# Local transformer: score masks written by ScalarE, and value windows read from a transposed copy of the state in DRAM

## The chip, the cores and the metric

The kernel runs on one core of one Trainium2 chip. The metric is the device time of one execution in microseconds (us), given as the median of three runs. Engines are named as in the profile: PE (TensorE, with its weight loader PEld), DVE (VectorE), ACT (ScalarE), POOL (GpSimd) and SP (SyncE, which only issues DMAs here).

## The reference

A model of two blocks over 16 sequences of 256 tokens with 128 channels, in f32. Block 0 has a linear attention and then, as its "ffn", a local transformer of six layers; block 1 has an attention with a position bias and a gelu MLP. The change lies in the local transformer:

```python
for i in range(6):                       # DEPTH
    x = attn_layer(shift_tokens(x), Wqkv[i], q_scale[i], k_scale[i], Wo[i]) + x
    x = ffn_layer(shift_tokens(x), ln_g[i], ln_b[i], W1[i], b1[i], W2[i], b2[i]) + x

def local_attention(q, k, v):            # 16 heads of 64, windows of 32 tokens
    bq, bk, bv = (t.reshape(b, h, n // 32, 32, 64) for t in (q, k, v))
    bk2, bv2 = look(bk), look(bv)        # own window and the one before: 64 keys
    mask = (it < jb) | (it > jb + w) | (jb == -1)
    sim = jnp.einsum('bhwie,bhwje->bhwij', bq, bk2) * 8.0
    sim = jnp.where(mask, -jnp.finfo(sim.dtype).max, sim)
    return jnp.einsum('bhwij,bhwje->bhwie', jax.nn.softmax(sim, -1), bv2)
```

Ahead of it q and k are divided by their norms, scaled and rotated; behind it the heads are multiplied by Wo and added to x.

## The kernel before, in words

There are three stages: the linear attention (0 to about 263 us), the local transformer (about 265 to 3640 us), and block 1 (from 3641 us). In the second stage the state lies transposed in SBUF: channels on the partitions, tokens along the row. A *unit* is two sequences; there are 8 units (`NU`), 6 layers (`DEPTH`), and each unit and layer is done in 4 iterations (`QS`), of four heads each: 192 iterations (`N`) of one loop (L1050 to L1129). It is a software pipeline: iteration n works on several lags at once.

For PE, ACT, DVE and POOL the order is the order of the code (`manual_schedule`); SP's DMAs, all in one queue, are ordered by the scheduler. In an iteration PE does, in order:

- `merging` (L927): output of iteration n-9 times the product of Wv and Wo (`vos`), 32 matmuls into the bank `y`; after the fourth of a unit the result is added to the state;
- `norms_rows` (L774, odd n): one transpose that turns the inverse norms of k into rows; ACT copies them out (`rkT`, L776), and a DMA brings them to DRAM (`rkh`);
- the steps of the feed-forward of an earlier unit (`ffn`, from L953 on, called through `behind`); its three gelus (L991) run on ACT at n%4 = 2, with a table load ahead of them and another ahead of the next exponentials;
- `flipped(p, 0)` (L888): four transposes of probabilities of iteration n-5; ACT copies them out (`prT`, L896);
- `windows` (L805), when n%4 = 3 for sequence s = 0 and when n%4 = 1 for s = 1: eight transposes of 64 tokens each, in steps of 32, so that the overlapping key blocks of 64 lie on partitions 0 to 63; ACT (L812) and DVE (L810) copy four each, and a DMA of 256 KB (L813) doubles them onto partitions 64 to 127;
- `masked` (L821): two matmuls of an identity with the bf16 mask, which open the two PSUM banks (`sim`) that the scores of iteration n-4 are added to;
- `flipped(p, 1)` (L888; DVE copies, L894);
- `norms_sum` (L722, even n): sums of squares of q and k; ACT copies them out (`n2`, L731);
- `weighted` (L906): 16 matmuls of windows and probabilities of iteration n-8; ACT and DVE copy out (`zx`, L921, L919);
- `scores` (L843): 128 small matmuls of iteration n-4 into the two `sim` banks; DVE takes the maxima (L855, L857);
- `norms_inverse` (L740, even n; the inverse square root runs on POOL, L758 to L766);
- `project` (L698): four matmuls for q and k of iteration n, each followed by a square on ACT (L701) and two DVE operations (L703, L706).

ACT interleaves with these the 16 exponentials of iteration n-4 (L865, with bias -max and an accumulated sum): eight for x = 0 between the squares, eight for x = 1 behind them. POOL divides by the sums (`divided`, L880, for x = 0 and x = 1), scales k by its inverse norms (`scaled`, L795) and adds the rotated halves (`rotate`, L714), which SP's eight `got` DMAs per iteration (L708, L709) bring. `widened` loads the inverse norms, spread over 64 partitions, as `kn` (four DMAs per iteration). PSUM has four banks for general use (`bank()`, named `mm`), three for `sim`, one for `y`. In the last iterations of a layer the next layer's Wq and Wk are loaded (`wqk`) and Wv and Wo multiplied (`merged`, L669 on).

Of the kernel before, what the change touches and what calls it, by code (L numbers as in the profile page):

```python
# [10 lines left out]
F32 = mybir.dt.float32  # L11
# [7 lines left out]
B, L, D = 16, 256, 128  # L19
NU = B // 2  # L20
# [4 lines left out]
WIN = 32  # L25
PAD = WIN
# [18 lines left out]
def adaln_kernel(  # L45
# [5 lines left out]
    nc = tc.nc  # L51
# [6 lines left out]
    def bank():  # L58
        return stage["ps"].tile([128, 512], F32, tag="mm", name="mm")
# [48 lines left out]
    zs = []  # L108
# [129 lines left out]
    with block:  # L238
# [98 lines left out]
        def upright(rows):  # L337

            pt = bank()
            for t in range(4):  # L340
                nc.tensor.transpose(pt[:, t * 128 : (t + 1) * 128], rows[:, t, :], ident)
            return pt
# [257 lines left out]
    with ExitStack() as es:  # L600
# [12 lines left out]
        def persistent(tag, shape, dtype=F32):  # L613
            t = lc.tile(list(shape), dtype, tag=tag, name=tag)
            nc.gpsimd.memset(t, 0.0)
            return t
# [7 lines left out]
        nc.sync.dma_start(sel, io["c_sel"])  # L624

        ks = [persistent(f"k{j}", (128, 2, PAD + L)) for j in range(8)]
        rope = lc.tile([128, 2, 2, L], F32, tag="rope", name="rope")
        nc.sync.dma_start(rope, io["c_rope"].rearrange("p (j a) t -> p j a t", j=2))

# [164 lines left out]
            k = ks[m % 8][:, :, PAD:]  # L794
            nc.gpsimd.tensor_tensor(k, k, two(kn), ALU.mult)  # L795

        def windows(u, s):


            xw = atile("xw", (128, 8, 128))  # L800
            for g in range(2):
                pt = bank()
                for j in range(4):
                    w0 = 32 * (4 * g + j)
                    nc.tensor.transpose(  # L805
                        pt[0:64, j * 128 : (j + 1) * 128], zs[u][:, s, w0 : w0 + 64], ident
                    )
                dst = xw[0:64, 4 * g : 4 * g + 4, :].rearrange("p w d -> p (w d)")
                if g:
                    nc.vector.tensor_copy(dst, pt[0:64, :])  # L810
                else:
                    nc.scalar.copy(dst, pt[0:64, :])  # L812
            nc.sync.dma_start(xw[64:128], xw[0:64])  # L813
            return xw

        def masked():

            sims = []
            for par in range(2):
                sim = pss.tile([128, 512], F32, tag="sim", name="sim")  # L820
                nc.tensor.matmul(  # L821
                    sim,
                    ident16,
                    maskb.unsqueeze(1).to_broadcast([128, 2, 256]),
                    start=True,
                    stop=False,
                    skip_group_check=True,
                )
                sims.append(sim)
            return sims  # L830

        def scores(sims, m, qs):

# [216 lines left out]
        while n < N + 9 or behind:  # L1050
            layer, at_ = divmod(n, per)
            if at_ == 13 and 0 < layer < DEPTH:
                wffs[layer] = load_ffn(layer)
            if 0 <= n - 4 < N:
                for m in (2 * (n - 4), 2 * (n - 4) + 1):
                    scaled(m, kns.pop(m))

            w, j = divmod(n - 9, QS)
            if 0 <= w < DEPTH * NU:
                if j == 0:  # L1060
                    pys[w] = psy.tile([128, 512], F32, tag="y", name="y")
                merging(j, zxs.pop((w, j)), vos[w // NU], pys[w])
                if j == QS - 1:
                    add_to_state(w % NU, pys.pop(w))
            if n % 2 and 3 <= n <= N + 1:
                home = norms_rows(rk)
            go_on(behind)
            go_on(merges)
            if 0 <= n - 1 < N:
                for m in (2 * (n - 1), 2 * (n - 1) + 1):  # L1070
                    rotate(m, qs[m], got.pop(m))
            if 0 <= n - 5 < N:
                i, u, p = place(n - 5)
                if p == 0:
                    prTs[i, u] = atile("prT", (128, NP, 512))
                flipped(p, 0, prs[n - 5], prTs[i, u])
            for s, lag in ((0, 7), (1, 9)):
                v, r = divmod(n - lag, QS)
                if r == 0 and 0 <= v < DEPTH * NU:
                    xws[v, s] = windows(v % NU, s)  # L1080
            sims = masked() if 0 <= n - 4 < N else None
            if 0 <= n - 5 < N:
                flipped(p, 1, prs.pop(n - 5), prTs[i, u])

            if n % 2 == 0 and 2 <= n <= N:
                n2 = norms_sum([squares.pop(m) for m in range(2 * n - 4, 2 * n)])
            v, r = divmod(n - 8, QS)
            if 0 <= v < DEPTH * NU:
                zxs[v, r] = weighted(r, xws[v, r // 2], prTs[v // NU, v % NU])
            go_on(behind)  # L1090
            if sims:
                m = 2 * (n - 4)
                rn = inverses[m // 4][:, m % 4 // 2]
                scores(sims, m, [qs.pop(m), qs.pop(m + 1)])
                pr = atile("pr", (128, 2, 4, 2, 64), 1)
                nbs = [maxima(sims[par], rn[:, par]) for par in range(2)]
                ssum = small("ssum", (128, 2, 4, 2))

            if n % 2 == 0 and 2 <= n <= N:
                rk, inverses[n // 2 - 1] = norms_inverse(n2)  # L1100
            if 0 <= w < DEPTH * NU and j == QS - 1:
                behind.append(ffn(w % NU, w // NU))
            go_on(behind)
            between = exponentials(0, sims, nbs, rn, pr, ssum) if sims else iter(())
            for m in (2 * n, 2 * n + 1):
                if n < N:
                    i, u, p = place(n)
                    qs[m], squares[m], got[m] = project(i, u, m, wqk[p + m % 2], between)
                if m % 2 == 0:
                    go_on(behind)  # L1110
            if sims:
                for x in range(2):
                    for _ in between:
                        pass
                    divided(pr[:, x], ssum[:, x])
                    between = exponentials(1, sims, nbs, rn, pr, ssum) if x == 0 else iter(())
                prs[n - 4] = pr
            if 0 <= n - 3 < N:
                for m in (2 * (n - 3), 2 * (n - 3) + 1):
                    kns[m] = widened(m, home)  # L1120
            if layer + 1 < DEPTH:
                if at_ == 18:
                    merges.append(merged(layer + 1))
                if at_ > per - QS:
                    p = 2 * (at_ - (per - QS) - 1)
                    wqk[p : p + 2] = [load_qk(layer + 1, p), load_qk(layer + 1, p + 1)]
            if at_ == 0 and 0 < layer < DEPTH:
                wqk[NP - 2 :] = [load_qk(layer, NP - 2), load_qk(layer, NP - 1)]
            n += 1  # L1129
# [468 lines left out]
```

## Time and profile before

| what | value |
| --- | --- |
| median of 3 runs (lowest to highest) | 4208.09 us (4206.36 to 4209.53) |
| the profiled execution: its time, its span | 4207.77 us, 4206.0 us |
| mean granted TensorE clock | 0.981 |
| second stage, 265 to 3640 us: busy PE, DVE, ACT, POOL | 3205.6, 2326.9, 2266.9, 2262.6 us of 3375 |
| PE on the windows' transposes (L805), one of 64 x 128 | 768, of about 0.11 us each when they follow each other |
| PE on the masks (L821) | 384, of 0.215 us each when they follow each other |
| DMA `xw<-xw` | 96 of 256 KB |

A line of the timeline gives start, duration, engine, line, operation, output <- inputs, partitions x elements, count, and in brackets how long the engine had been idle and what released it. In a line of groups the numbers after the bar are busy time and mean duration in ns of one, and after the next bar the idle time just before these instructions with its releaser. The granted clock is that of PE, 1.00 at full speed.

### The profile page before, as it was taken

How to read it: one execution, taken by the hardware profiler on the slowest of the kernel's cores; microseconds unless marked ns; L12 is line 12 of the kernel's file. 1: busy time of each engine (PE TensorE's matmuls, PEld its weight loads, DVE VectorE, ACT ScalarE, POOL GpSimd, SP SyncE). 2: the span in 40 equal slices, each digit the busy share in tenths (PEclk: the TensorE clock that was granted, in tenths of full speed). 3: DMA queues.
4: the chain of work that ended last, by engine and by line, in shares of the span. 5: the costliest groups of instructions: out<-in, count | busy, mean ns of one | idle time of the engine just before them, and what ended most of it. 6: DMA issues, size and time to landing. Idle time of an engine off the chain costs nothing.

```text
span 4206.0 us, 118202 instructions
## 1 busy us (share of the span) xinstructions
PE 3938.9 (94%) x45491; PEld 2580.1 (61%) x45491; DVE 2856.0 (68%) x6005; ACT 2753.1 (65%) x9640; POOL 2655.1 (63%) x3374
## 2 busy tenths in 40 slices
PE   7877999999999999999999999999999999799998
PEld 4534666666666666666666666666666666455554
DVE  6746767677767767676777777776767675476664
ACT  4535666667666666667666667666666766276665
POOL 5446666776666676666676766767666665155453
PEclk9878999999999999999999999999999999899999
DMA  1333444444444444444444444444434442200000
GB/s 41 41 90 97 106 109 105 109 107 105 106 105 114 104 110 105 105 110 102 111 109 105 112 103 106 108 110 105 110 100 105 104 105 72 64 1 6 9 3 11
DMA packets 193547, 371.06 MB, mean 88 GB/s; under 512 B 42537, under 2 KB 83416, under 8 KB 192984
## 3 DMA queue, kind: packets, MB, share of 16 engines
q1 hardware_dynamic: 192984, 363.50, 34.3%
q8 instruction: 360, 5.90, 0.6%
q14 instruction: 203, 1.66, 0.1%
HBM read 127.92 MB, written 8.91 MB: 33 GB/s over the span
## 4 chain that ended last, share of the span: by engine, by line
PE 46%; DVE 22%; ACT 19%; issue 7%; POOL 5%; DMA 1%; SPq 0%; POOLq 0%; DVEq 0%; ACTq 0%
ACT pr L865 11%; PE mm L906 9%; PE sim L843 7%; DVE sent L703 6%; ACT sq L701 4%; PE mm L722 4%; PE mm L888 4%; POOL pr L880 4%; DVE k L706 3%; DVE q L706 3%; PE mm L698 3%; DVE mx L855 3%; PE mm L805 2%; PE mm L1376 2%; PE sim L1303 2%
## 5 line engine op out<-in xcount | busy, mean ns | idle before, releaser
L865 ACT ACTIVATE pr<-sim,nb,rq 128x64 f32<-128x64 f32 x3072 | 1229.5, 454 | 336.8 <-DVE nb L857 318.3
L880 POOL TENSOR_TENSOR pr<-pr,rsum 128x512 f32<-128x512 f32 x384 | 398.3, 1042 | 807.3 <-DVE rsum L878 761.8
L865 ACT ACTIVATION_READ_ACCUMULATOR pr<-sim,nb,rq 128x1 f32 x3072 | 784.5, 255 | 0.0
L927 PEld LDWEIGHTS y<-zx,wvo 128*128 128x128 f32 x6144 | 716.1, 192 | 92.1 <-issue 89.0
L927 PE MATMUL y<-zx,wvo 128*128 128x128 f32 x6144 | 717.7, 275 | 1.3 <-ACT zx L921 1.2
L698 PE MATMUL mm<-z,wqk 128*128 128x512 f32 x1536 | 706.9, 602 | 8.6 <-DMA wqk<-in_L_ffn_Wqkv_dram 6.7
L703 DVE SCALAR_TENSOR_TENSOR sent<-mm,vec,rope 128x512 f32<-128x512 f32 x768 | 570.4, 743 | 118.2 <-ACT sq L701 110.2
L714 POOL TENSOR_TENSOR q<-q,got 128x512 f32<-128x512 f32 x384 | 488.3, 1272 | 12.7 <-DMA got<-sent 10.2
L714 POOL TENSOR_TENSOR k<-k,got 128x512 f32<-128x512 f32 x384 | 496.2, 1292 | 0.0
L795 POOL TENSOR_TENSOR k<-k,kn 128x512 f32<-128x512 f32 x384 | 481.9, 1274 | 17.9 <-DMA kn<-rkh 17.9
L701 ACT ACTIVATE sq<-mm 128x512 f32<-128x512 f32 x768 | 475.7, 619 | 23.3 <-PE mm L698 23.3
L698 PEld LDWEIGHTS mm<-z,wqk 128*128 128x128 f32 x1536 | 278.7, 192 | 322.9 <-issue 234.7
L919 DVE COPY zx<-mm 128x512 f32<-128x512 f32 x384 | 265.6, 692 | 262.0 <-PE mm L906 262.0
L921 ACT COPY zx<-mm 128x512 f32<-128x512 f32 x384 | 224.9, 586 | 287.0 <-PE mm L906 287.0
L906 PE MATMUL mm<-prT,xw 64*128 64x256 f32 x3072 | 389.7, 391 | 3.8 <-DVE zx L919 2.0
L855 DVE TENSOR_REDUCE mx<-sim 128x8 f32<-128x512 f32 x384 | 263.1, 685 | 171.9 <-PE sim L843 171.9
L906 PEld LDWEIGHTS mm<-prT,xw 64*128 64x128 f32 x3072 | 293.5, 187 | 121.7 <-issue 92.2
L1346 POOL TENSOR_TENSOR pr<-pr,rsum 128x256 f32<-128x256 f32 (+1 forms) x256 | 205.1, 832 | 241.7 <-DVE rsum L1344 218.3
L888 PE MATMUL mm<-ident,pr 128*128 128x128 f32 x1536 | 244.6, 282 | 105.1 <-POOL pr L880 75.9
L888 PEld LDWEIGHTS mm<-ident,pr 128*128 128x128 f32 x1536 | 174.9, 142 | 270.0 <-POOL pr L880 240.6
L843 PEld LDWEIGHTS sim<-k,q 64*32 64x32 f32 x24576 | 265.8, 105 | 83.3 <-issue 55.2
L843 PE MATMUL sim<-k,q 64*32 64x64 f32 x24576 | 299.7, 226 | 15.9 <-POOL k L795 8.1
(253 smaller groups left out, 6461.5 us busy)
## 6 DMA issues: line engine op xcount, KB each, us to landing
got<-sent SPq DMA_DIRECT2D x1536, 128.0 KB
kn<-rkh SPq DMA_DIRECT2D x768, 128.0 KB
xw<-xw SPq DMA_DIRECT2D x96, 256.0 KB
wqk<-in_L_ffn_Wqkv_dram SPq DMA_DIRECT2D x48, 128.0 KB
bhome<-brow SPq DMA_DIRECT2D x1, 3072.0 KB
wv<-in_L_ffn_Wqkv_dram SPq DMA_DIRECT2D x12, 256.0 KB
wo<-in_L_ffn_Wo_dram SPq DMA_DIRECT2D x12, 256.0 KB
xt<-in_x_dram SPq DMA_DIRECT2D x8, 256.0 KB
```

Source lines behind the costliest of these rows:

```text
L698: nc.tensor.matmul(pp, wqk[:, j, :], xs, start=True, stop=True)
L701: nc.scalar.activation(sq, pp, AF.Square)
L703: nc.vector.scalar_tensor_tensor(two(sent[:, j, :]), two(pp), scale, tab[1], ALU.mult, ALU.mult)
L714: nc.gpsimd.tensor_tensor(r, r, two(got[:, j, :]), ALU.add)
L795: nc.gpsimd.tensor_tensor(k, k, two(kn), ALU.mult)
L843: nc.tensor.matmul(sims[par][32 * c : 32 * c + 32, c0 : c0 + 64], q[r, s, t0 : t0 + 32], k[r, s, t0 : t0 + 64], start=False, stop=True, sk ...
L855: nc.vector.tensor_reduce(mx, sim.rearrange("p (b k) -> p b k", b=8), AX.X, ALU.max)
L865: nc.scalar.activation(pr[:, x, st, par, :], sims[par][:, b * 64 : (b + 1) * 64], AF.Exp, bias=nbs[par][:, b : b + 1], scale=rn[:, par, b ...
L880: nc.gpsimd.tensor_tensor(prf, prf, rsum.unsqueeze(2).to_broadcast([128, 8, 64]), ALU.mult)
L888: nc.tensor.transpose(pt[:, st * 128 : (st + 1) * 128], pr[:, x, st].rearrange("p h k -> p (h k)"), ident,)
L906: nc.tensor.matmul(pz[par][:, w * 256 : (w + 1) * 256], xw[r, (2 * k + w) % 8, :], prT[r, :, 64 * k + 32 * w : 64 * k + 32 * w + 32], star ...
L927: nc.tensor.matmul(py[:, j * 128 : (j + 1) * 128], vo[:, h, :], zx[:, h % 2, h // 2, :], start=(h == 0), stop=(h == 2 * NP - 1), skip_grou ...
```

## The change

Two things change in the second stage.

*Masks.* `masked` now handles one `sim` bank per call, and only the first three calls of all (the ring's three banks) use the matmul; the other 381 are an ACT copy of the bf16 mask into the bank, and the scores are added to what lies there. It is called one iteration ahead of the scores: the first bank behind `flipped(p, 1)` (on ACT: behind the prT copy and ahead of n2 and zx), the second at the end of the iteration (on ACT: behind all exponentials, ahead of the next iteration's rkT, gelu and prT work).

*Windows.* Once per unit and layer (n%4 = 3) `upright` transposes the state of both sequences by four 128x128 transposes into one bank, ACT copies it out, and two DMAs of 128 KB write it as rows into a DRAM buffer (one of two, by unit), behind 32 rows of zeros. `windows` then makes no transposes: four DMAs of 128 KB per sequence read the overlapping blocks of 64 rows straight onto both halves of the partitions. In `before` a unit has sixteen transposes, two ACT and two DVE copies and two DMAs for it. A memset and four small DMAs at the stage's start write the zeros.

In the built order of SP, the loads of `kn` in the iteration n%4 = 3 change place too: three of the four now come behind the eight `got` DMAs, where before they alternated.

```diff
--- before.py
+++ after.py
@@ -624,6 +624,13 @@
         nc.sync.dma_start(sel, io["c_sel"])
 
         ks = [persistent(f"k{j}", (128, 2, PAD + L)) for j in range(8)]
+
+        rows = [dr.tile([2, PAD + L, D], F32, tag=f"rows{j}", name=f"rows{j}") for j in range(2)]
+        zero = work("zero")[0:PAD, 0:D]
+        nc.vector.memset(zero, 0.0)
+        for home in rows:
+            for s in range(2):
+                nc.sync.dma_start(home[s, 0:PAD, :], zero)
         rope = lc.tile([128, 2, 2, L], F32, tag="rope", name="rope")
         nc.sync.dma_start(rope, io["c_rope"].rearrange("p (j a) t -> p j a t", j=2))
 
@@ -794,40 +801,48 @@
             k = ks[m % 8][:, :, PAD:]
             nc.gpsimd.tensor_tensor(k, k, two(kn), ALU.mult)
 
-        def windows(u, s):
+        def upright(u, home):
+
+            pt = bank()
+            for t in range(4):
+                s, c = t // 2, PAD + 128 * (t % 2)
+                nc.tensor.transpose(
+                    pt[:, t * 128 : (t + 1) * 128], zs[u][:, s, c : c + 128], ident
+                )
+            xt = work("xt").rearrange("p (s h d) -> p s h d", s=2, h=2)
+            nc.scalar.copy(xt.rearrange("p s h d -> p (s h d)"), pt)
+            for s in range(2):
+                nc.sync.dma_start(
+                    home[s, PAD : PAD + L, :].rearrange("(h p) d -> p h d", p=128), xt[:, s]
+                )
+
+        def windows(s, home):
 
 
             xw = atile("xw", (128, 8, 128))
-            for g in range(2):
-                pt = bank()
-                for j in range(4):
-                    w0 = 32 * (4 * g + j)
-                    nc.tensor.transpose(
-                        pt[0:64, j * 128 : (j + 1) * 128], zs[u][:, s, w0 : w0 + 64], ident
-                    )
-                dst = xw[0:64, 4 * g : 4 * g + 4, :].rearrange("p w d -> p (w d)")
-                if g:
-                    nc.vector.tensor_copy(dst, pt[0:64, :])
-                else:
-                    nc.scalar.copy(dst, pt[0:64, :])
-            nc.sync.dma_start(xw[64:128], xw[0:64])
+            for r in range(0, 128, WIN):
+                t0 = r % (2 * WIN)
+                nc.sync.dma_start(
+                    xw[r : r + WIN],
+                    home[s, t0 : t0 + L, :].rearrange("(w p) d -> p w d", p=WIN),
+                )
             return xw
 
+
+
+        banks = []
+
         def masked():
 
-            sims = []
-            for par in range(2):
-                sim = pss.tile([128, 512], F32, tag="sim", name="sim")
+            sim = pss.tile([128, 512], F32, tag="sim", name="sim")
+            src = maskb.unsqueeze(1).to_broadcast([128, 2, 256])
+            if len(banks) < 3:
                 nc.tensor.matmul(
-                    sim,
-                    ident16,
-                    maskb.unsqueeze(1).to_broadcast([128, 2, 256]),
-                    start=True,
-                    stop=False,
-                    skip_group_check=True,
-                )
-                sims.append(sim)
-            return sims
+                    sim, ident16, src, start=True, stop=False, skip_group_check=True
+                )
+            else:
+                nc.scalar.copy(sim.rearrange("p (x c) -> p x c", x=2), src)
+            banks.append(sim)
 
         def scores(sims, m, qs):
 
@@ -1077,10 +1092,14 @@
             for s, lag in ((0, 7), (1, 9)):
                 v, r = divmod(n - lag, QS)
                 if r == 0 and 0 <= v < DEPTH * NU:
-                    xws[v, s] = windows(v % NU, s)
-            sims = masked() if 0 <= n - 4 < N else None
+                    if s == 0:
+                        upright(v % NU, rows[v % 2])
+                    xws[v, s] = windows(s, rows[v % 2])
             if 0 <= n - 5 < N:
                 flipped(p, 1, prs.pop(n - 5), prTs[i, u])
+            if 0 <= n - 3 < N:
+                masked()
+            sims = banks[2 * (n - 4) : 2 * (n - 3)] if 0 <= n - 4 < N else None
 
             if n % 2 == 0 and 2 <= n <= N:
                 n2 = norms_sum([squares.pop(m) for m in range(2 * n - 4, 2 * n)])
@@ -1116,6 +1135,7 @@
                     between = exponentials(1, sims, nbs, rn, pr, ssum) if x == 0 else iter(())
                 prs[n - 4] = pr
             if 0 <= n - 3 < N:
+                masked()
                 for m in (2 * (n - 3), 2 * (n - 3) + 1):
                     kns[m] = widened(m, home)
             if layer + 1 < DEPTH:
```

## The prediction

> **What bounds the kernel now.** I read the page first: busy shares, the slices, the chain, the groups.
>
> ```profile
> PE 3938.9 (94%) x45491; PEld 2580.1 (61%) x45491; DVE 2856.0 (68%) x6005; ACT 2753.1 (65%) x9640; POOL 2655.1 (63%) x3374
> PEclk9878999999999999999999999999999999899999
> ...
> PE 46%; DVE 22%; ACT 19%; issue 7%; POOL 5%; DMA 1%; SPq 0%; POOLq 0%; DVEq 0%; ACTq 0%
> ...
> L888 PEld LDWEIGHTS mm<-ident,pr 128*128 128x128 f32 x1536 | 174.9, 142 | 270.0 <-POOL pr L880 240.6
> ```
>
> 94% looks like a kernel bound by TensorE, and a change that takes TensorE work away looks good. But a busy matmul here includes its waiting in the pipeline, and the chain is only 46% PE. The last line is the key: before the transposes of the probabilities (L888) the weight loader stands idle for 270 us, 241 of them for POOL's division (L880). So I read one quiet spot in time order, PE and POOL, at the iteration with n%4 = 1 of one unit:
>
> ```profile
> 1348.63 0.83 PE L927 MATMUL y<-zx,wvo 128*128 128x128 f32 x6
> 1349.31 0.27 PE L774 MATMUL mm<-ident,rk 128*32 128x128 f32 x1
> 1349.41 0.95 PE L962 MATMUL mm<-mean,fs 128*128 128x1 f32 x8
> 1351.13 0.66 PE L888 MATMUL mm<-ident,pr 128*128 128x128 f32 x4 [0.76 <-POOL pr L880]
> 1351.62 1.04 PE L805 MATMUL mm<-ident,z 128*64 128x128 f32 x8
> 1352.50 0.59 PE L821 MATMUL sim<-maskb,ident 128*128 128x512 bf16 x2
> 1352.93 0.60 PE L888 MATMUL mm<-ident,pr 128*128 128x128 f32 x4
> 1353.46 2.00 PE L906 MATMUL mm<-prT,xw 64*128 64x256 f32 x16
> ```
> ```profile
> 1350.03 1.04 POOL L880 TENSOR_TENSOR pr<-pr,rsum 128x512 f32<-128x512 f32 x1 [2.23 <-DVE rsum L878]
> 1351.66 1.04 POOL L880 TENSOR_TENSOR pr<-pr,rsum 128x512 f32<-128x512 f32 x1 [0.58 <-DVE ve L970]
> ```
>
> POOL's second division ends at 1352.70; the second L888 starts at 1352.93. Window transposes (L805) and masks (L821), all that the change takes from PE here, lie between the two L888, in time in which PE would otherwise wait for POOL. The stage (265 to 3640 us, 192 iterations) is a loop of latencies: scores, maxima, sixteen exponentials on ACT, the division on POOL, the second L888, weighted, scores again. Its period is not the sum of PE's work.
>
> **The change, part by part.** I took the four iterations of the unit from 1300 to 1368 us and compared the second L888's start with what else it must wait for. Periods from L888 to L888 are 19.22, 14.94, 17.82 and 15.63 us, 67.6 a unit.
>
> *n%4 = 1:* the second L888 could start, by the tightest such pair (0.055 us, at n%4 = 0), 0.055 after the division instead of 0.23: **−0.17 us**.
>
> *n%4 = 3:* the gap from POOL's division (ends 1318.58) to the second L888 (1319.59) is 1.01 us: eight L805 and two L821 stand in it. The first L888 waits there for ACT's rkT copy (it ends at 1317.25, L888 starts at 1317.39), and the change puts a mask copy ahead of that one, 0.48 us. So: first L888 at 1317.87, plus 0.53 for its four, plus 0.5 for four 128x128 window transposes of the same size, second L888 at 1318.9, weighted 0.53 later, near 1319.48 (its bank is freed by DVE's gating L1003 at 1319.38) instead of 1320.12: **−0.64**.
>
> *n%4 = 0:* already 0.055 behind the division: **0**.
>
> *n%4 = 2:* here the feed-forward's gelu table load starts on ACT at 1298.24, right behind the last exponential; the norms' matmuls (L722) start at 1300.93, after the second gelu. The second mask copy of each iteration is placed behind the exponentials, so ahead of this load; the gelus and L722 queue behind it. The trace has no ACT write to PSUM and no bf16 source; the nearest rows are ACT copies of 128x512 out of PSUM, 0.585 us each and 0.48 from start to start, and a Square from SBUF to SBUF (L958) at 0.647. The copy can start at 1298.01, 0.38 behind the start of the last exponential, and end between 1298.49 and 1298.66; the load then starts 0.25 to 0.42 later than now. Nearest to the copies' own length: **+0.38**. The Trainium skill bears on this one: "ScalarE: Activation LUTs" (the tip on ScE→PSUM) has ACT writing to PSUM faster than to SBUF; no run here shows it, and by it the term would sit at its lower bound, 48 x 0.13 = 6 us less in all.
>
> Sum: −0.43 a unit, x48 = **−21 us**. The first mask copy of an iteration stands behind the prT copy, where ACT now idles until weighted gives it a bank (1.74 us ahead of the zx copy at 1354.62); it costs nothing while that cover is there, and 0.5 an iteration without it. What is late next where a stall goes is POOL's division everywhere.
>
> *Layer turns.* In some three iterations of each turn the merged weights are multiplied in as well and PE is the bound. There the saving counts whole: two masks at 0.215 us (0.43) and a quarter of twelve transposes at 0.11 (0.33), 0.76 x 3 x 5 turns = **−11 us**. Base: −32.
>
> *Queues.* SP now issues, per unit, two row writes and eight reads where two copies stood, some 0.55 us each; three of the four loads of kn in iteration n%4 = 3 come behind eight rotations (`got`). They then issue 13.9 to 15.7 us after the second L888, land in 3.05 (the median here), and POOL's scaling ends near 19.5 instead of 17.4, 0.5 us before the scores need it. I count 0; should a load take 4.0 (the 90th percentile) it would be +0.5 a unit, 24 us. The windows arrive two DMAs later (about 3.4 + 3.1 us), but weighted needs them a whole iteration later. The start adds a memset and four small DMAs, below 0.5 us once.
>
> **The clock.** This decides the sign. From 411.69 to 3534.88 the granted clock is 1.00; just before, in the stage's start, and just after, in its drain, it halves, always on a grid of 3.41 us. I read PE in such stretches (columns: stretch, length, PE busy and matmuls, granted clock, DMA share, GB/s):
>
> ```profile
> 404.86:408.28 3.42, 1.63 (x10) 1.00 0.78 177
> 408.28:411.69 3.41, 3.41 (x18) 0.50 0.13 48
> 439.00:442.41 3.41, 1.69 (x13) 1.00 0.77 175
> 1349.31:1352.72 3.41, 2.65 (x25) 1.00 0.78 178
> 2510.93:2514.35 3.42, 2.66 (x26) 1.00 0.76 175
> 3531.47:3534.88 3.41, 2.15 (x19) 1.00 0.00 0
> 3534.88:3538.30 3.42, 3.10 (x14) 0.50 0.02 5
> ```
>
> Thin stretches are followed by half clock (404.86, 3531.47), but busy time does not sort them: 439.00 kept its clock with less than 3531.47. So I count columns sent. Two masks follow each other in 0.215 us per 512 columns, 0.42 ns each: a mask is 0.215 us, a 128-column transpose 0.053, one of L962's single columns nothing. 3531.47 is the same spot of the loop: 3 of L927, the rkT transpose, 4 of L888, 3 of L805 begin in it, 0.59 us: it fell. 404.86 holds 8 of L888 and 2 masks, 0.85: fell; 439.00 adds the first of L722: stayed. 2510.93 holds some 18 of 128 columns, 0.95: stayed. I estimate the edge at 0.6 to 0.9. The spot at 1349.31 holds rkT, 4 of L888, 8 of L805, 2 masks, 0.05 + 0.21 + 0.43 + 0.43 = 1.1. Without the last two terms it is **0.26**, below anything that stayed.
>
> The spot from merging's end (1349.3) to weighted (then at 1353.29) is 4.0 us, longer than a stretch. With merging sending 0.053 per 0.117 us and weighted 0.107 per 0.125, starts of a stretch from about 1348.6 to 1350.1 (edge 0.6) or 1348.1 to 1350.4 (edge 0.85) fall: 1.5 to 2.3 of each 3.41 us. A unit of 67.2 us is 19 x 3.41 + 2.3, or 20 stretches less 1.1: unit by unit the grid moves by 1.1 through that zone; a hit unit is 1.5 us longer and moves by only 0.4, so it tends to be hit again. I take **two units in three**. The price: the next 3.41 us run at half clock. Sixteen weighted matmuls took 3.88 us so (from 3583.46) against 2.00 here, the sixteen of L722 3.57 (from 408.33) against 1.92: 1.65 us lost where a half-clock stretch is full of such work. As it starts between 1351.5 and 1353.8 it lies over the second L888, weighted and the scores, with some waiting in the earliest. I take 1.5, all of it on the loop. 43 units (48 less those at a turn, where merging fills the spot) x 0.66 x 1.5 = **+43 us**.
>
> The Trainium skill has two rules on it. "TensorE: Matmul & The Clock Gate", its section "Why this matters for your kernels", asks for no idle gap of PE over about 3 us; taken word by word it lets this change pass, since four transposes stand in the middle of the stretch, and the time would be that without the clock term. Its "Part 4: PE-mode transpose" says that transposes don't count as busy in the same way; then the spot would be quieter still; all 43 units hit would be 64, 4240 in all. The stretch at 3531.47 fell although its longest wait of PE is under 1 us, so I go by the rows.
>
> **Sum:** 4207.8 (this execution; median 4208.1, so no correction) − 32 + 43 = **4219 us**.
>
> **Rivals.**
> 1. *No clock loss* (the edge lies below 0.26 us of columns, or not columns but something else decides). For: only two stretches of this stage fell, and the columns are my reading of them. Against: that the one of the drain held twice what will be left. Time 4208 − 32 = 4176 (4164 to 4196).
> 2. *PE-bound after all*: all removed work counts. 8 x 0.215 + 12 x 0.11 = 3.04 a unit x 48 = 146: 4062. Against: the 241 us that the loader waits for POOL.
> 3. *Slower still*: one mechanism, late kn. If the loads behind the eight rotations take over 3.5 us, POOL's scaling ends after the scores want it, and from there each us counts in each unit: +0.5 x 48 = 24, 4243 with the clock term; with every unit hit, 4265.
> 4. *It does not do what it says*: masks stay on PE. The built order shows three mask matmuls left and 381 copies on ACT, so this is a remainder; no change, 4208.
>
> **How the numbers follow.** Forecast 0.52, rival 1 0.25, rival 2 0.03, rival 3 0.16, rival 4 0.04. The forecast's own range is 4199 to 4240 (hits from 0.45 to 0.9 of the units, price 1.2 to 1.7). A time within 0.2% (4199.7 to 4216.5) cannot be told from no change here. Faster: 0.05 of the forecast, 0.23 of rival 1, 0.03: 0.31. Same: 0.15 + 0.02 + 0.04 = 0.21. Slower: 0.32 + 0.16 = 0.48. The range, 4168 to 4260, leaves out rival 2, the lower part of rival 1 and the worst of rival 3, below 0.2.
>
> **What would show it.** Right: granted clock below 1.00 in stretches of the stage, weighted's sixteen at up to 3.9 us once in most units, behind n%4 = 1; more waiting for POOL ahead of the second L888 (half a us and more an iteration); L722 still waiting for the gelu, 0.3 to 0.6 later; the mask copy at 0.48 to 0.65 on ACT. Wrong: the clock stays at 1.00 (then 4176), or POOL's scaling waits for kn beyond 20 us after the second L888 of n%4 = 3 (then above 4240), or the second L888 waits for something other than POOL.

## The result, and the profile after

The changed kernel takes 4254.68 us (median of 4 runs, 4247.72 to 4254.96) against 4208.27 us: a ratio of 1.0107, 95% interval 1.0089 to 1.0124. The profiled execution took 4247.72 us, 39.9 us more than the one of before (4207.77 us). Its page:

```profile
PE 3844.1 (91%) x44534; PEld 2509.1 (59%) x44534; DVE 2840.9 (67%) x5910; ACT 2924.1 (69%) x9973; POOL 2660.5 (63%) x3374
...
PEclk9888999999999999999999999999999999899999
...
PE 34%; ACT 30%; DVE 14%; issue 7%; POOL 6%; SPq 5%; DMA 4%; ACTq 0%; POOLq 0%; DVEq 0%
...
L802 POOL TENSOR_TENSOR k<-k,kn 128x512 f32<-128x512 f32 x384 | 483.4, 1276 | 127.3 <-DMA kn<-rkh 117.5
...
L903 PEld LDWEIGHTS mm<-ident,pr 128*128 128x128 f32 x1536 | 166.1, 144 | 374.0 <-POOL pr L895 358.6
```

Lines of the changed kernel are numbered 7 to 20 higher. PE is busy 95 us less, and the weight loader waits 118 us more for POOL ahead of the probabilities' transposes (L903): the work taken away has become waiting. PE's share of the chain falls from 46 to 34%. New is the wait of POOL's scaling (L802) for `kn`, 117.5 us instead of 17.9. The granted clock looks full in slices of 106 us.

At finer grain, the clock fell exactly where the prediction looked for it. First the stretches of 3.41 us at one such spot, then PE's timeline there:

```profile
1353.00:1356.38 3.38, 3.38 (x30) 1.00 0.25 60
1356.38:1359.80 3.42, 2.27 (x20) 1.00 0.88 201
1359.80:1363.21 3.41, 3.18 (x14) 0.50 0.28 72
```
```profile
1356.93 0.27 PE L781 MATMUL mm<-ident,rk 128*32 128x128 f32 x1
1357.04 0.95 PE L977 MATMUL mm<-mean,fs 128*128 128x1 f32 x8
1358.99 0.65 PE L903 MATMUL mm<-ident,pr 128*128 128x128 f32 x4 [1.00 <-POOL pr L895]
1360.03 1.11 PE L903 MATMUL mm<-ident,pr 128*128 128x128 f32 x4 [0.39 <-POOL pr L895]
1361.08 3.03 PE L921 MATMUL mm<-prT,xw 64*128 64x256 f32 x16
```

The stretch from 1356.38 sends little; in the next the clock is 0.50, and weighted (L921) takes 3.03 us instead of 2.00. But from 440 to 3440 us the trace has only nine such stretches, all in this spot, in 9 of 44 units and not in two of three.

To see where the rest is I took every iteration's median from the traces, from its scores to the next scores (column 0 holds the exponentials of n%4 = 0 and the second L888 of n%4 = 1, and so on). *Quiet unit* is the sum of the four, without halved iterations where these are the most; *mean unit* takes in the layer turns and halvings (iterations 30 to 180 of 0 to 191, counted by their scores). *Halved stretches* counts the 3.41 us at half clock from 440 to 3440 us. All but the last column are of the profiled execution.

| kernel | 0 | 1 | 2 | 3 | quiet unit | mean unit | halved stretches | median, us |
| --- | --- | --- | --- | --- | --- | --- | --- | --- |
| before | 15.87 | 17.52 | 17.34 | 16.89 | 67.62 | 68.31 | 0 | 4208 |
| after | 16.41 | 18.13 | 16.46 | 17.36 | 68.36 | 69.06 | 9 | 4255 |
| masks_only | 15.77 | 18.13 | 16.67 | 17.10 | 67.67 | 68.58 | 2 | 4220 |
| windows_only | 16.18 | 17.65 | 16.82 | 17.48 | 68.13 | 68.69 | 6 | 4225 |
| kn_first | 15.75 | 18.14 | 16.19 | 17.62 | 67.70 | 69.05 | 23 | 4235 |
| kn_moved | 15.75 | 17.65 | 16.67 | 17.62 | 67.69 | 69.07 | 28 | 4224 |
| before_hand | 15.87 | 17.53 | 17.35 | 16.90 | 67.65 | 68.30 | 0 | 4198 |
| before_split | 15.86 | 18.11 | 16.96 | 16.91 | 67.84 | 69.05 | 2 | 4236 |
| hold | 15.75 | 17.64 | 16.66 | 17.62 | 67.67 | 68.42 | 6 | 4207 |
| hold_split | 15.87 | 17.95 | 16.28 | 16.96 | 67.06 | 68.28 | 11 | 4198 |
| nb_before | 15.86 | 17.57 | 16.94 | 16.88 | 67.25 | 67.76 | 0 | 4175 |
| nb_hold | 15.78 | 17.54 | 16.25 | 16.70 | 66.27 | 67.68 | 11 | 4161 |
| late_before | 16.77 | 18.18 | 17.34 | 16.89 | 69.18 | 69.61 | 1 | 4265 |
| nb_hold2 | 15.74 | 17.54 | 16.24 | 16.68 | 66.20 | 67.22 | 4 | 4145 |

### The profile page after: what moved, and what is told of

The parts are those of the page before. It is cut to its first block, busy times and chain, and to the rows that moved or that the text cites. A ratio compares the mean times of both kernels' runs of the same rounds, so it can differ in the third digit from the quotient of the medians.

```text
span 4245.9 us, 117219 instructions
## 1 busy us (share of the span) xinstructions
PE 3844.1 (91%) x44534; PEld 2509.1 (59%) x44534; DVE 2840.9 (67%) x5910; ACT 2924.1 (69%) x9973; POOL 2660.5 (63%) x3374
## 4 chain that ended last, share of the span: by engine, by line
PE 34%; ACT 30%; DVE 14%; issue 7%; POOL 6%; SPq 5%; DMA 4%; ACTq 0%; POOLq 0%; DVEq 0%
ACT pr L880 18%; PE mm L921 8%; PE sim L858 6%; ACT sq L708 6%; PE mm L903 3%; POOL pr L895 3%; PE mm L729 3%; DVE sent L710 3%; DVE mx L870 3%; DMA xw<-rows 3%; PE mm L1396 2%; SPq L793 2%; PE sim L1323 2%; DVE nb L872 2%; PE mm L1386 2%
## 5 line engine op out<-in xcount | busy, mean ns | idle before, releaser
L880 ACT ACTIVATION_READ_ACCUMULATOR pr<-sim,nb,rq 128x1 f32 x3072 | 762.3, 248 | 0.0
L705 PE MATMUL mm<-z,wqk 128*128 128x512 f32 x1536 | 715.7, 605 | 22.8 <-DVE fx L970 12.9
L802 POOL TENSOR_TENSOR k<-k,kn 128x512 f32<-128x512 f32 x384 | 483.4, 1276 | 127.3 <-DMA kn<-rkh 117.5
L721 POOL TENSOR_TENSOR q<-q,got 128x512 f32<-128x512 f32 x384 | 489.1, 1274 | 13.9 <-DMA got<-sent 10.4
L903 PE MATMUL mm<-ident,pr 128*128 128x128 f32 x1536 | 253.8, 289 | 225.4 <-POOL pr L895 131.1
L921 PE MATMUL mm<-prT,xw 64*128 64x256 f32 x3072 | 424.4, 405 | 5.7 <-DVE zx L934 3.9
L921 PEld LDWEIGHTS mm<-prT,xw 64*128 64x128 f32 x3072 | 321.5, 195 | 127.4 <-issue 55.0
L903 PEld LDWEIGHTS mm<-ident,pr 128*128 128x128 f32 x1536 | 166.1, 144 | 374.0 <-POOL pr L895 358.6
```

What stands on the lines that cost most here:

```text
L705: nc.tensor.matmul(pp, wqk[:, j, :], xs, start=True, stop=True)
L721: nc.gpsimd.tensor_tensor(r, r, two(got[:, j, :]), ALU.add)
L880: nc.scalar.activation(pr[:, x, st, par, :], sims[par][:, b * 64 : (b + 1) * 64], AF.Exp, bias=nbs[par][:, b : b + 1], scale=rn[:, par, b ...
L903: nc.tensor.transpose(pt[:, st * 128 : (st + 1) * 128], pr[:, x, st].rearrange("p h k -> p (h k)"), ident,)
L921: nc.tensor.matmul(pz[par][:, w * 256 : (w + 1) * 256], xw[r, (2 * k + w) % 8, :], prT[r, :, 64 * k + 32 * w : 64 * k + 32 * w + 32], star ...
```

## The experiments

The first theory, from the two traces alone (L): late `kn` costs 1.0 us a unit, the mask copy ahead of the gelu 0.5, some ten halvings 15 us, against gains of 0.9 and 0.17 us. Its rival was the forecast's own sum (C): the clock does most of it.

**masks_only**: the kernel before with the mask part of the diff (`masked()` on ACT, called twice an iteration), windows as before.

> The masks' part alone: ScalarE writes the masks, the windows stay as before. Two theories of the 46 us by which the changed kernel is slower. Theory L (from its trace: late loads of kn cost about 1.0 us a unit, the mask copy ahead of the gelu table load 0.5 to 0.6 us a unit, halved clock stretches 10 x 1.5 us, against gains of 0.9 us at n%4 = 3 and 0.17 at n%4 = 1): here the kn loads keep their place, the eight window transposes still stand in the spot, and only the gelu's delay (48 x 0.55 = 26) and -8 at n%4 = 1 and some -5 at the layer turns are left: about 4220 us (4210 to 4230). Theory C (the forecast's: the clock does most of it): the spot at n%4 = 1 holds 0.69 us of columns instead of 1.1, at the edge, so half the units or more lose 1.5 us: 4240 to 4260, with over 20 halved stretches in the stage.

4220.5 us, ratio 1.0025 (1.0013 to 1.0037), two halved stretches. The time is L's, the reason is not: iteration 1 is 0.61 us longer, as L had it, but the quiet unit is the same as before to 0.05 us. What is lost behind the gelu comes back one iteration later. The mean unit is 0.27 us longer. In the trace, iterations 8 to 184 are 13 us longer in all: some 3 of them in the quiet units, 5 at the layer turns, where both halved stretches lie, and 5 in single iterations that were not followed.

**windows_only**: the window part of the diff alone (`rows`, `upright`, the four reads each), masks by PE.

> The windows' part alone: one transposition a unit and the way through DRAM, masks by TensorE as before. The kn loads stand behind the rotations as in the changed kernel. Theory L: +48 us for late kn, nothing for the gelu, gains of about 0.7 us at n%4 = 3 and 0.17 at n%4 = 1 (-42), some clock loss (0 to 10): about 4216 us (4206 to 4228), with POOL's scaling waiting some 2 us a unit for kn. Theory C: 0.69 us of columns in the spot, so 4190 to 4215 from the gains and a clock loss of 20 to 40, and no cost from kn. If kn cost nothing and the clock held, 4166.

4225.2 us, ratio 1.0044 (1.0027 to 1.0061), with POOL waiting for `kn` 74 us in 2400, some 2 us a unit. As L had it, though this run alone does not show that late `kn` is the price; the next run takes the wait away.

**kn_first**: the whole change with SyncE's order by hand, `kn` ahead of the rotations.

```diff
-        es.enter_context(tc.manual_schedule(engines=ENGINES))
+        es.enter_context(tc.manual_schedule(engines=ENGINES | {mybir.EngineType.SP}))
...
+            if 0 <= n - 3 < N:
+                for m in (2 * (n - 3), 2 * (n - 3) + 1):
+                    kns[m] = widened(m, home)
             between = exponentials(0, sims, nbs, rn, pr, ssum) if sims else iter(())
...
-                for m in (2 * (n - 3), 2 * (n - 3) + 1):
-                    kns[m] = widened(m, home)
```

> The whole change, but SyncE's order is written out by hand: in each iteration the four kn loads come behind the row writes and window reads and ahead of the eight rotations, in all iterations. Nothing else differs. Theory L: the 1.0 us a unit of late kn goes, so about 4250 - 48 = 4203 us (4192 to 4215), and POOL's wait for kn falls from 117 us to under 20. Theory C: within 6 us of the changed kernel, 4245 to 4258.

4235.2 us, ratio 1.0064 (1.0049 to 1.0079). POOL's wait for `kn` is gone (1.6 us in all), and the quiet unit falls from 68.36 (68.28 without halved iterations) to 67.70; but the kernel gains 20 us, not 48, and has 23 halved stretches instead of 9. Both theories miss: the unit comes back to that of before and no lower, though iteration 2 has become 1.15 us shorter.

**kn_moved**: kn_first with both mask copies behind the prT copy, none ahead of the gelu.

```diff
-            if 0 <= n - 3 < N:
-                masked()
+            for k in (n - 4, n - 3):
+                if 0 <= k < N:
+                    masked()
...
-            if 0 <= n - 3 < N:
-                masked()
```

> As kn_first, and both mask copies of an iteration stand behind the prT copy (the second one of this iteration's scores, then the first one of the next's), so none is ahead of the gelu table load or the rkT copy. Theory L: another 0.5 us a unit at n%4 = 2 goes, and at n%4 = 3 the rkT copy comes 0.5 us earlier: kn_first less 25 to 40 us, about 4170 (4155 to 4185). Theory C: the spot is as empty as before, so 4240 to 4255.

4223.9 us, ratio 1.0041 (1.0028 to 1.0055); neither theory had it. The gelu's 0.5 us is gone from iteration 1, and 0.48 us has come up in iteration 2. The quiet unit does not move by 0.02 us. Something that none of these edits touches sets it.

The timelines show it, at n%4 = 3. First GpSimd's from the second division on, then VectorE's of the maxima and `nb`, in the kernel before:

```profile
1317.54 1.04 POOL L880 TENSOR_TENSOR pr<-pr,rsum 128x512 f32<-128x512 f32 x1 [0.47 <-DVE rsum L878]
1318.54 2.51 POOL L795 TENSOR_TENSOR k<-k,kn 128x512 f32<-128x512 f32 x2
1321.02 1.26 POOL L714 TENSOR_TENSOR q<-q,got 128x512 f32<-128x512 f32 x1
1322.25 1.27 POOL L714 TENSOR_TENSOR k<-k,got 128x512 f32<-128x512 f32 x1
1323.49 1.25 POOL L714 TENSOR_TENSOR q<-q,got 128x512 f32<-128x512 f32 x1
```
```profile
1323.79 0.69 DVE L855 TENSOR_REDUCE mx<-sim 128x8 f32<-128x512 f32 x1 [0.90 <-PE sim L843]
1324.51 0.26 DVE L857 SCALAR_TENSOR_TENSOR nb<-mx,rq 128x8 f32<-128x8 f32 x1
```

The same two views of kn_first:

```profile
900.81 1.05 POOL L895 TENSOR_TENSOR pr<-pr,rsum 128x512 f32<-128x512 f32 x1 [0.48 <-DVE rsum L893]
901.82 2.50 POOL L802 TENSOR_TENSOR k<-k,kn 128x512 f32<-128x512 f32 x2
904.28 1.27 POOL L721 TENSOR_TENSOR q<-q,got 128x512 f32<-128x512 f32 x1
905.52 1.26 POOL L721 TENSOR_TENSOR k<-k,got 128x512 f32<-128x512 f32 x1
906.75 1.25 POOL L721 TENSOR_TENSOR q<-q,got 128x512 f32<-128x512 f32 x1
```
```profile
906.15 0.69 DVE L870 TENSOR_REDUCE mx<-sim 128x8 f32<-128x512 f32 x1 [0.67 <-PE sim L858]
906.88 1.16 DVE L872 SCALAR_TENSOR_TENSOR nb<-mx,rq 128x8 f32<-128x8 f32 x1
```

`nb`, 128x8, takes 0.17 us when GpSimd is idle. Here it takes 0.26 and 1.16, and ends within 0.04 us of the end of the third rotation (1324.74 and 908.00) in both. Behind the division the scores come 0.7 us earlier in kn_first, and `nb` only waits longer. In the kernel before, from 600 to 3000 us, 179 of 282 `nb` take over 0.2 us, and every one of these ends within 0.05 us of the end of a GpSimd operation. From the end of the second division to the end of the next first `nb`, in us:

| kernel | 0 | 1 | 2 | 3 |
| --- | --- | --- | --- | --- |
| before | 5.35 | 7.42 | 6.18 | 7.41 |
| kn_first | 5.37 | 7.44 | 6.18 | 7.42 |
| hold | 5.36 | 7.42 | 6.16 | 7.42 |
| nb_before | 5.39 | 7.05 | 6.16 | 6.93 |
| nb_hold | 5.28 | 6.91 | 5.25 | 6.98 |

Two scalings (2.5 us) and three or four rotations (1.24 each) are 6.2 and 7.5 us; in column 0 it is two scalings, two operations of the feed-forward (1.0 and 0.6) and one rotation, 5.4, not two rotations as the expectation of nb_before has it. So the loop runs over POOL (division, scalings, rotations) to `nb`; the second L888, weighted and scores run beside it. Theory P: `nb` is held by the running GpSimd operation. The Trainium skill has the rule: "SBUF — State Buffer", section "Who interferes with whom", says that a VectorE instruction with two SBUF inputs contends with a GpSimd instruction that reads SBUF. `nb` has two (mx and the inverse norms), and the traces agree; that the wait lasts to the end of a GpSimd operation is read from the rows above.

**before_hand**, the control: the kernel before with kn_first's diff.

> A control: the kernel before with SyncE's order written out by hand as in kn_first (rkT row, window copy, four kn loads, eight rotations, in every iteration). Both theories: no change, 4208 +- 5 us, and no halved stretch in the stage.

4198.4 us, ratio 0.9979 (0.9969 to 0.9988), 10 us less than the kernel before. The quiet unit is the same. In the profiled executions most of it lies at the stage's start: the scores of iteration 8 begin at 439.7 us instead of 446.2; from there to iteration 184 the two differ by 0.7 us. The kernels with the hand order are compared with this one.

**before_split**: GpSimd's operations cut in two.

```diff
-                nc.gpsimd.tensor_tensor(r, r, two(got[:, j, :]), ALU.add)
+                for s in range(2):
+                    nc.gpsimd.tensor_tensor(r[:, s], r[:, s], two(got[:, j, :])[:, s], ALU.add)
...
-            nc.gpsimd.tensor_tensor(k, k, two(kn), ALU.mult)
+            for s in range(2):
+                nc.gpsimd.tensor_tensor(k[:, s], k[:, s], two(kn)[:, s], ALU.mult)
```

> The kernel before, with GpSimd's rotations and scalings of 128x512 cut into two of 128x256 each; nothing else. Theory P (new, from the traces so far: VectorE's 128x8 operation nb, 0.17 us when GpSimd is idle, ends 0.02 us after the GpSimd operation that was running when it started, up to 1.2 us later; so it can only come in between two of them, and time won ahead of it is given back there): the wait is halved, and 10 to 40 us go, 4170 to 4200, with nb's mean falling from 0.41 to below 0.32 us. Without P: unchanged or some us slower by the added instructions, 4205 to 4225.

4236.0 us, ratio 1.0070 (1.0055 to 1.0085): wrong in size and sign. Each half takes 0.73 us, so GpSimd has 0.85 us more to do in an iteration (2817.9 us busy instead of 2655.1, over 192), and `nb` does not get in at the first gap: of 224 long waits 121 lasted over the ends of two or three halves. Theory P stands as far as GpSimd holds `nb`; that `nb` comes in at the next gap does not hold for short operations.

**hold**: kn_moved with PE writing both masks at n%4 = 1, in the spot.

```diff
+            if n % 4 == 1:
+                for k in (n - 4, n - 3):
+                    if 0 <= k < N:
+                        masked(True)
             if 0 <= n - 5 < N:
                 flipped(p, 1, prs.pop(n - 5), prTs[i, u])
-            for k in (n - 4, n - 3):
-                if 0 <= k < N:
-                    masked()
+            if n % 4 != 1:
+                for k in (n - 4, n - 3):
+                    if 0 <= k < N:
+                        masked()
```

> As kn_moved, but in iterations n%4 = 1 both masks are written by TensorE, between the two transpositions of the probabilities, where they stood in the kernel before; in the other three they stay on ScalarE. Clock part of the theory (each halved stretch behind n%4 = 1 costs 1.5 to 2.2 us, kn_moved had some 25): the spot holds 0.69 us of columns instead of 0.26, most halvings go (under 8 left), and 4224 falls to 4180 (4168 to 4195). If the clock loss were hidden by another wait, 4215 to 4225.

4206.5 us, ratio 0.9996 (0.9987 to 1.0006); halved stretches fall from 28 to 6, the time by 17 us. Giving PE 0.43 us of work a unit back makes the kernel faster. The edit takes two copies off ACT as well, but the quiet unit does not feel it (67.69 and 67.67). The kernel ends 8 us above before_hand, with the same quiet unit (67.67 and 67.65): without late `kn` and with little clock loss the change gains nothing.

**hold_split**: hold with before_split's diff.

> hold with the cut GpSimd operations of before_split. Theory P: the time won at n%4 = 3 is no longer given back at nb of the next iteration: 20 to 40 us below hold, about 4150 (4130 to 4172). Without P: as hold or a few us slower.

4198.3 us (4184 to 4219), ratio 0.9982 (0.9965 to 0.9999): 8 us below hold, not 20 to 40. Iteration 3 falls from 17.62 to 16.96, as P has it, iteration 1 grows by 0.3, and eleven stretches are halved. Both expectations missed, and it is inconclusive by itself.

**nb_before**: before_hand with the maxima in PSUM, so that `nb` reads SBUF once.

```diff
-            mx = small("mx", (128, 8))
...
-                nbs = [maxima(sims[par], rn[:, par]) for par in range(2)]
+                pm = bank()
+                nbs = [maxima(sims[par], rn[:, par], pm[:, 8 * par : 8 * par + 8]) for par in range(2)]
```

> before_hand (the kernel before with SyncE's order by hand, 4198 us), with the row maxima mx written to a PSUM bank instead of SBUF, so that nb has one SBUF input instead of two; nothing else. Theory P (from the traces: in every kernel the time from the end of GpSimd's second division to the end of the next nb is the same, 7.42, 6.18, 7.41 and 5.36 us in the four iterations, that is two scalings and four, three, four or two rotations, whatever PE does beside them; nb waits there until a GpSimd operation ends): nb takes 0.17 us everywhere, the four waits of 0.2 to 0.55 us go, and the kernel falls by 50 to 80 us, to about 4135 (4115 to 4155). Rival (nb's length is only the same wait seen twice, or the operand does not matter): 4190 to 4205.

**nb_hold**: hold with the same edit.

> hold (the whole change, with kn in time, masks away from the gelu and the clock held, 4206 us), with mx in PSUM in the same way. Theory P: here nb waited longer at n%4 = 3 (1.16 us), so more goes: 80 to 115 us, to about 4105 (4090 to 4130), and it ends 20 to 45 us below nb_before: the 32 us of the forecast's base gain, which the wait had swallowed. If the change gains nothing even then, it ends within 10 us of nb_before. Rival as for nb_before: 4195 to 4210.

4174.6 us, ratio 0.9921 (0.9905 to 0.9938), and 4161.1 us, ratio 0.9891 (0.9876 to 0.9906). The groups of `nb` from 600 to 3000 us, in hold and in nb_hold (count, busy, mean ns):

```profile
L872 DVE SCALAR_TENSOR_TENSOR nb<-mx,rq 128x8 f32<-128x8 f32 x280 | 140.4, 501 | 9.6
```
```profile
L871 DVE SCALAR_TENSOR_TENSOR nb<-mm,rq 128x8 f32<-128x8 f32 x284 | 47.4, 167 | 9.7
```

Every one is now 0.167 us long, with GpSimd running as before: the second SBUF input was the cause. The gains, 24 and 45 us, are about half of what I expected or less. In nb_before `nb` ends 0.5 us earlier in iteration 0, and the exponentials end 11.73 us after the start of the scores instead of 11.75: they alternate with the squares of the projections, and these are next (read from the order, not tested). Only iteration 2 is shorter, by 0.41. But with `nb`'s wait gone the change, in the form that it has in hold, is worth something: 66.27 against 67.25 us, 0.98 a quiet unit or 47 us in 48. 13.5 us of it are left: eleven stretches are halved (nine of them in the spot, 18 us), and at five places, the layer turns, PE waits 10.8 us in all for the bank that now holds the maxima.

**late_before**: before_hand with three of the four `kn` loads of n%4 = 3 behind the eight rotations' DMAs, as in the changed kernel.

> before_hand with the kn loads in the changed kernel's place in iteration n%4 = 3 alone: one ahead of the eight rotations' DMAs, three behind them; nothing else. Late kn costs 0.5 us a unit: 4198 + 24 = 4222 (4212 to 4234), with GpSimd's scaling waiting some 2 us a unit for kn. If kn is hidden as the forecast had it: 4195 to 4203.

4265.3 us, ratio 1.0138 (1.0123 to 1.0153): 67 us, far over the 24. POOL waits for `kn` as in the changed kernel (117.5 us there), and the timelines of PE and POOL show why it costs more here:

```profile
L795 POOL TENSOR_TENSOR k<-k,kn 128x512 f32<-128x512 f32 x384 | 482.4, 1274 | 119.2 <-DMA kn<-rkh 116.6
```
```profile
1016.45 0.66 PE L888 MATMUL mm<-ident,pr 128*128 128x128 f32 x4 [1.00 <-POOL pr L880]
1016.95 1.04 PE L805 MATMUL mm<-ident,z 128*64 128x128 f32 x8
1017.82 0.59 PE L821 MATMUL sim<-maskb,ident 128*128 128x512 bf16 x2
1018.25 0.60 PE L888 MATMUL mm<-ident,pr 128*128 128x128 f32 x4
```
```profile
1015.36 2.09 POOL L880 TENSOR_TENSOR pr<-pr,rsum 128x512 f32<-128x512 f32 x2 [1.40 <-DVE rsum L878]
1017.41 2.51 POOL L795 TENSOR_TENSOR k<-k,kn 128x512 f32<-128x512 f32 x2
```

Late scaling delays the rotations, and the fourth then holds another short operation of VectorE: `ny` (128x64, a step of the inverse root, L751) takes 0.195 us in every unit of before_hand and 1.09 in 32 of 43 here, ending 0.05 us after a rotation. In the changed kernel it looks the same:

```profile
798.08 1.27 POOL L721 TENSOR_TENSOR k<-k,got 128x512 f32<-128x512 f32 x1
798.32 1.08 DVE L758 TENSOR_SCALAR ny<-nx 128x64 int32<-128x64 int32 x1
```

What stands behind it on VectorE is late, the first eight exponentials end later, and the two divisions follow each other at once. The first L888 starts 1.0 us ahead of the second division's end instead of 1.6, and windows and masks (1.3 us) push the second to 0.8 us behind it instead of 0.2. So the scores start 3.3 us behind the division instead of 2.7 (medians), `nb` misses the end of a rotation and waits for the next one: 6.6 us from the division to its end, where before_hand has 5.4. In the changed kernel, with the spot empty, these two are 2.6 and 5.4 in spite of the late `kn`. The emptied spot does buy something, but only against a delay that the change itself makes.

**nb_hold2**: nb_hold with each mask of n%4 = 1 written twice by PE.

```diff
-                nc.tensor.matmul(
-                    sim, ident16, src, start=True, stop=False, skip_group_check=True
-                )
+                for _ in range(2 if pe else 1):
+                    nc.tensor.matmul(
+                        sim, ident16, src, start=True, stop=False, skip_group_check=True
+                    )
```

> nb_hold with each of the two TensorE masks of n%4 = 1 written twice into its bank (the second write replaces the first), so that the spot again holds 1.1 us of columns, as in the kernel before, instead of 0.69; nothing else. It adds TensorE work and takes none away. Clock theory: the 13 halved stretches of nb_hold go (0 to 2 left), each worth 1.3 to 2 us: 4161 - 20 = 4141 (4133 to 4148). If halvings cost nothing on this loop, or if columns do not hold the clock: 4159 to 4167.

4144.9 us, ratio 0.9846 (0.9829 to 0.9864): two useless matmuls a unit make the kernel 16 us faster, with 4 halved stretches instead of 11. In the spot none of 45 units is left, where nb_hold had nine; the four lie at layer turns. It is the fastest version here, 64 us below the kernel before.

## Why the prediction was right, and where it was not

The direction was right and 4254.7 lies in the range of 4168 to 4260, with some luck: it lies outside the forecast's own range (4199 to 4240), and the range reaches as far as that only for rival 3. The forecast of 4219 was 36 us low; two terms of its sum, which nearly cancel, and one zero were off.

- **Base, −32: about −5 came.** The step that failed is "What is late next where a stall goes is POOL's division everywhere". I compared each second L888 with the division ahead of it, and did not follow POOL beyond that: its scalings and rotations hold `nb`. Of the −21 of the quiet units nothing came through (kn_first 67.70, before 67.62). The mask copy took 0.57 to 0.73 us, and L888 did come 0.6 us later behind the gelu, but that too lay beside POOL's run. The gains were there and were swallowed: with `nb`'s wait gone, nb_hold is shorter than nb_before by 0.69 us in iteration 2 and by 0.08 in iteration 0, where −0.64 and −0.17 were forecast. Of the −11 at the layer turns about half came: the eight iterations around each turn are, in all five, 25.8 us longer than quiet ones in the kernel before and 20.4 in the changed one, leaving out halved iterations and the ones behind them. The lines were there: `nb` at 1324.51 took 0.26 us and others up to 1.1 us, mean 0.41, for eight elements a row.
- **Queues, "I count 0": about 25 us.** The issue times were nearly right (14.6 to 15.9 us after the second L888 for 13.9 to 15.7), but the scaling ends at 20.6 (median), not at 19.5: the sign that I had given for rival 3. I set its margin against the scores alone. The rotations behind it have none: the fourth holds `ny`, which takes 1.09 us in 30 of 44 units and 0.195 in every one of the kernel before and of kn_first. Without halved iterations the quiet unit is 0.58 us longer than kn_first's (68.28 and 67.70). My rival 3 named late `kn` with the wrong point from which it decides.
- **Clock, +43: the mechanism was right, the count was not; 10 us came.** Spot, stretch and the slower weighted are those predicted (1359.80). In the 3.41 us ahead of each of the nine halved stretches PE's longest wait is 1.0 us, so the Trainium skill's wording by idle gaps ("TensorE: Matmul & The Clock Gate", "Why this matters for your kernels") would have passed them. The share of two units in three went with a unit of 67.2 us. With late `kn` the unit is some 68.3 us, and 20 stretches are 68.27: the grid hardly moves from unit to unit. By where weighted starts on the grid, the nine hits lie from 0.5 us ahead of a stretch's start to 1.3 behind it, and 30 of the 44 units lie outside that. With the unit at 67.7 (kn_first, kn_moved) 23 and 28 stretches fell, some of them two in a row, in 19 and 18 of 44 units, where I had 28 of 43. The price, read from the halved iterations and the ones behind them less the medians of the others, is 10 us for the nine, 35 for kn_first's 23, 41 for kn_moved's 28, 8.5 for hold's six and 18 for the nine of nb_hold: 1.1 to 2.0 us a stretch, around the 1.5. With 0.26 us of columns in the spot 19 and 18 of 44 units fell where `kn` was in time (kn_first, kn_moved); with 0.69, none (masks_only) to 11 (hold_split); with 1.1, none (before, before_hand, nb_before, nb_hold2, late_before) or one (before_split). The prediction's own rows (0.85 fell, 0.95 stayed) put the edge for a stretch at 0.85 to 0.95, not at 0.6 to 0.9.
- **Sum of the profiled execution.** From the scores of iteration 8 to those of iteration 184 it is 30.2 us longer: 28.6 in the quiet units (0.65 each, 44 units), 10.3 around the halved stretches, less 5.4 at the layer turns and 3.4 in other iterations. The start adds 1.4, and from iteration 184 to the end it is 8.3, for which the forecast had no term; together 39.9. The other executions took 7 us more. One of these (4254.71) has the same granted clock, 0.974, so halvings alone do not seem to make this difference; it is open.

Open too: what makes the end of the stage longer, and the single iterations of masks_only.

## What to carry to other kernels

Work taken from an engine where it waits between two steps of a loop buys nothing there, and the engine that it waits for need not set the period by that step either: follow that one through the work that it does next, and look for a short operation of a third engine whose duration varies. Compare that duration with its shortest; the difference is a wait that no list of waits shows. When work is taken out of an engine whose granted clock falls behind thin stretches, count what is left in the thinnest one, and when DMAs are added to one queue, find out which of the old ones they push back.

## What the runs showed of the hardware

- A VectorE operation of 128x8 with two SBUF inputs took 0.167 us or up to 1.3 us, ending 0.02 us after a GpSimd operation; with one input in PSUM it took 0.167 us in all 284 cases. With GpSimd operations of 0.73 us one behind the other it had to let two or three pass in 121 of 224 long waits.
- One SBUF input is not always enough: `ny`, a VectorE operation of 128x64 with one, took 0.195 us, or 1.09 whenever it started while a rotation ran (30 of 44 units of the changed kernel).
- Two more matmuls a unit, without use, made a kernel 16 us faster, by holding the granted clock: nine of 45 spots fell without them, none with them.
- ScalarE's write of a bf16 mask into PSUM took 0.57 to 0.73 us for 128x512 (median 0.65), no less than its copies from PSUM to SBUF (0.59) or its Square from SBUF to SBUF (0.63 to 0.65); the tip of "ScalarE: Activation LUTs" in the Trainium skill, weighed in the prediction, that PSUM is the faster target does not show here.
